# The first grouped FFN's prelude rearranged: routing in single operations beside long and short units, shared outputs two tiles at a time, later groups' rows on ScalarE

## The chip, the core and the metric

The kernel runs on one core of a Trainium2 chip. The metric is the device time of one launch in microseconds (us). The core's engines work side by side, each through its own queue: TensorE (PE; PEld is its loading of weights), VectorE (DVE), ScalarE (ACT), GpSimd (POOL) and SyncE (SP). Indirect DMAs are issued from POOL, most others from SP.

## The reference

The input x has 8 x 512 rows of 256 float32 numbers. Six layers follow one another, each on the layernorm of x and added to x. The change touches the fourth, and a part that it shares with the sixth:

```python
x = x + 0.5 * _L0_ffn_ref(_layernorm(x, axis=-1), ...)   # experts choose rows
x = x + _L0_attn_ref(_layernorm(x, axis=-1), ...)
x = x + 0.5 * _L0_ffn_ref(_layernorm(x, axis=-1), ...)
x = x + 0.5 * _L1_ffn_ref(_layernorm(x, axis=-1), ...)   # first grouped FFN
x = x + _L1_attn_ref(_layernorm(x, axis=-1), ...)
x = x + 0.5 * _L1_ffn_ref(_layernorm(x, axis=-1), ...)   # second grouped FFN
```

In `_L1_ffn_ref` a gate gives each row a softmax over 16 experts. The 16 lie in 4 groups; the 2 groups with the largest best score stay, and of their experts the row takes the 4 best, weighted by their scores. An expert computes `silu(x w1) * (x w3)` with 128 columns, times `w2`. Every row also goes through one shared expert of the same form with 256 columns (`ws1`, `ws3`, `ws2`).

## The kernel before, in words

The 4096 rows are 32 tiles of 128 rows, in 8 groups of 4 tiles. x stays on chip from layer to layer, after the third layer by way of a table in DRAM (`acc_d`). `ffn1_before` (L2129) is the first grouped FFN. All of its engines run in the order in which the program issues (a manual schedule): what is written earlier stands earlier in the queue of its engine, and every instruction waits for those ahead of it in that queue. The rows are taken in two parts: part 0 is tiles 0 to 11 (groups 0 to 2), part 1 is tiles 12 to 31 (groups 3 to 7).

The prelude, for each part:

- Mean and variance of each tile on DVE (`ln_mean`, L184 to L187); the reciprocal root for several tiles at once, for group 0 by `ln_guess` (L195, twelve small operations on DVE with no square root), for all others by `ln_range` (L178: the square root on ACT at L192, the rest on DVE at L221 to L226).
- `normal` (L1657): the normalised rows, one DVE operation a tile (L1473), into a tile that the profile calls wide.
- `columns` (L1661): 8 transposes a group on PE (tp, L1667), copied by ACT into xnT (L1670).
- `logits` (L1672): 16 small matmuls a group against the gate's weights (lg, L1675).
- `routing` (L1496): a long chain of DVE operations on the scores of the whole part (192 numbers a partition in part 0, 320 in part 1): softmax with the exponential on ACT (L1507), `topk` (L1316) for groups and for experts, counts of rows for each expert by two matmuls (pb L1543, pa L1551), the slot of each row (`slot`, L1570), the expert of each slot tile (`owner`, L1578), and the weights (`coef`, L1579 to L1582).
- `send` (L1477): 4 indirect DMAs a tile from POOL, which put each row into the slots of its experts in DRAM (slots_d, L1482). Each send waits for the last but one. Part 0 has 48, part 1 has 80.

The shared expert is cut into units that are put between these steps so that PE has work. A hidden unit (L1696, 8 matmuls of 128x512 in the profile, Silu on ACT at L1702, a product on DVE at L1707) makes half of the hidden layer of a group; an output unit (yp, L1718, 4 matmuls of 128x256) makes one tile, and DVE adds it to x (L1724). `Pump` (L2108) holds the list. Its `run(n)` issues the PE part of n units; the DVE part of each unit is issued after the PE part of the next one. `routing` is a generator that stops at each `yield`; `advance(steps, n)` (L2097) lets it go on by n stops, fewer where it says "turn". So DVE's order in routing is 3 stops (part 0) or 2 (part 1), then the DVE part of a unit, and so on.

Behind the prelude come the tile steps (L1730): the slot tiles are loaded two at a time on SP (xs, L1743), transposed (tpx, L1755), put through their expert (hs L1769, tpa L1783, yps L1791) and stored (ys_d, L1798). Loads run 4 steps ahead, and a load waits for all sends of its part. While the steps of part 1 run, the results of part 0 are gathered back and added to x. Then the attention of the fifth layer begins (its first PE instruction is tpn, L1063). The second grouped FFN (`ffn1_after`, L2276, class `Joint`) uses the same shared units behind its own tile steps, with its own routing, whose first part is done during the attention.

Of the kernel before, what the change touches and what calls it, by code (L numbers as in the profile page):

```python
# [19 lines left out]
P = 128  # L20
# [49 lines left out]
class Kernel:  # L70
# [1245 lines left out]
    def topk(self, pool, vals, n, k, hots):  # L1316


        nc = self.nc
        T = vals.shape[1]  # L1320
        left = pool.tile([P, T, n], F32, name=f"left{n}")
        nc.vector.tensor_copy(left, vals)
        for r in range(k):
            m = pool.tile([P, T], F32, name="m", bufs=2)
            nc.vector.tensor_reduce(m, left, AX.X, ALU.max)
            yield
            if n == E1:
                rank = pool.tile([P, 2, T, n], F32, name="pick")[:, 0]
            else:
                rank = pool.tile([P, T, n], F32, name=f"rank{n}")  # L1330
            nc.vector.tensor_tensor(rank, left, bc(m, 2, n), ALU.is_equal)
            nc.vector.tensor_tensor(rank, rank, bc(self.desc[:, 0:n], 1, T), ALU.mult)
            yield
            m = pool.tile([P, T], F32, name="m", bufs=2)
            nc.vector.tensor_reduce(m, rank, AX.X, ALU.max)
            nc.vector.tensor_tensor(hots[:, r], rank, bc(m, 2, n), ALU.is_equal)
            yield
            if r < k - 1:
                nc.vector.scalar_tensor_tensor(left, hots[:, r], -2.0, left, ALU.mult, ALU.add)

# [111 lines left out]
class Grouped:  # L1452
# [43 lines left out]
    def routing(self, h, lg, pool, row_psum):  # L1496
# [8 lines left out]
        nc.vector.tensor_reduce(m, lg, AX.X, ALU.max)  # L1505
        nc.vector.tensor_tensor(score, lg, bc(m, 2, E1), ALU.subtract)
        nc.scalar.activation(score, score, AF.Exp)  # L1507
        m = pool.tile([P, HT], F32, name="m", bufs=2)
# [3 lines left out]
        nc.vector.tensor_tensor(score, score, bc(m, 2, E1), ALU.mult)  # L1512
        grouped = score.rearrange("p t (g j) -> p (t g) j", g=N_GROUPS)
# [16 lines left out]
        nc.vector.tensor_tensor(view, hots[:, 0], hots[:, 1], ALU.add)  # L1530
        nc.vector.tensor_tensor(view, view, hots[:, 2], ALU.add)
        yield
        nc.vector.tensor_tensor(view, view, hots[:, 3], ALU.add)

# [8 lines left out]
        nc.tensor.matmul(pb, lhsT=k.ones, rhs=chosen.rearrange(flat), start=True, stop=True)  # L1543
        inc = pool.tile([P, E1, HT], F32, name=f"left{E1}")
# [5 lines left out]
        pa = row_psum(E1 * HT)  # L1550
        nc.tensor.matmul(pa, lhsT=k.tri, rhs=chosen.rearrange(flat), start=True, stop=True)  # L1551
# [4 lines left out]
        base = pool.tile([P, E1], F32, name="base")  # L1556
        nc.vector.tensor_tensor(base, upto, tiles, ALU.subtract)
# [6 lines left out]
        for r in range(0, TOPK, 2):  # L1564
            pick = pool.tile([P, 2, HT, E1], F32, name="pick")
            nc.vector.tensor_tensor(
                pick, hots[:, r : r + 2], bc(inc.rearrange("p e t -> p t e"), 1, 2), ALU.mult
            )
            nc.vector.tensor_reduce(where[:, r : r + 2], pick, AX.X, ALU.add)
        nc.vector.tensor_copy(self.slot[h][:, :, :HT], where)  # L1570
# [4 lines left out]
        nc.vector.tensor_scalar(past, upto, k.lanes[:, 0:1], None, ALU.is_le, ALU.add, accum_out=number)  # L1575
        row = row_psum(P)
        nc.tensor.matmul(row[0:1, :], lhsT=number, rhs=k.ident, start=True, stop=True)
        nc.vector.tensor_scalar(self.owner[h][:, : self.tiles[h]], row[0:1, : self.tiles[h]], float(E1 - 1), None, ALU.min)  # L1578
        nc.vector.tensor_tensor(hots, hots, bc(score, 1, TOPK), ALU.mult)  # L1579
        yield  # L1580
        nc.vector.tensor_reduce(self.coef[h][:, :, :HT], hots, AX.X, ALU.add)
# [74 lines left out]

    def normal(self, g):  # L1657
        for t in range(g * QT, g * QT + QT):
            self.rows(self.k.nc.vector, self.xn[:, t, :], t)
# [20 lines left out]
    def row_psum(self, cols):  # L1680
        t = self.psum.tile([P, CH], F32, name="pp", tag="lg", bufs=1)
        return t[:, :cols]

    def shared(self, g):

        nc, x = self.k.nc, self.k.x
        SC = SHARED // P

        def hidden(s):
            hs = []  # L1690

            def pe():
                for wt in (self.ws1, self.ws3):
                    hp = self.psum.tile([P, CH], F32, name="hp", tag="h", bufs=2)
                    for c in range(DC):
                        nc.tensor.matmul(  # L1696
                            hp, lhsT=wt[:, c, s * P : s * P + P], rhs=self.xnT[g][:, c, :],
                            start=(c == 0), stop=(c == DC - 1),
                        )
                    hs.append(hp)  # L1700
                sg = self.work.tile([P, CH], F32, name="sg")
                nc.scalar.activation(sg, hs[0], AF.Silu)  # L1702
                hs.append(sg)

            def dve():
                at = self.acts[g, s] = self.work.tile([P, CH], F32, name="at", bufs=4)
                nc.vector.tensor_tensor(at, hs[2], hs[1], ALU.mult)  # L1707
            return pe, dve

        def outputs(i):  # L1710
            box = []
            t = g * QT + i

            def pe():
                yp = self.psum.tile([P, D], F32, name="yp", tag="y", bufs=2)
                box.append(yp)
                for c in range(SC):
                    nc.tensor.matmul(  # L1718
                        yp, lhsT=self.acts[g, c][:, i * P : i * P + P], rhs=self.ws2[:, c, :],
                        start=(c == 0), stop=(c == SC - 1),  # L1720
                    )

            def dve():
                nc.vector.scalar_tensor_tensor(x[:, t, :], box[0], 0.5, x[:, t, :], ALU.mult, ALU.add)  # L1724
            return pe, dve

        return [hidden(s) for s in range(SC)], [outputs(i) for i in range(QT)]
# [369 lines left out]
def advance(steps, n):  # L2097

    for _ in range(n):
        what = next(steps, "end")  # L2100
        if what == "end":
            return False
        if what == "turn":
            break
    return True


class Pump:  # L2108


    def __init__(self):
        self.units, self.pending = [], None
# [4 lines left out]
    def run(self, n):  # L2117
        for _ in range(n):
            if self.units:
                pe, dve = self.units.pop(0)  # L2120
                pe()
            else:
                dve = None
            if self.pending is not None:
                self.pending()
            self.pending = dve


def ffn1_before(k, f):  # L2129
# [3 lines left out]
    with ExitStack() as ctx, k.tc.manual_schedule(engines={E.PE, E.DVE, E.Activation, E.Pool, E.SP}):  # L2133
# [3 lines left out]
        a = f.parts[0]  # L2137
        lg = f.psum.tile([P, a, E1], F32, name="lg", tag="lg", bufs=1)
        for t in range(QT):
            k.ln_mean(f.route, f.stats, t)  # L2140
        k.ln_guess(f.route, f.stats, 0, QT)
        f.normal(0)
        f.columns(0)
        k.ln_range(f.route, f.stats, QT, a - QT)
        f.normal(1)
        f.normal(2)
        f.columns(1)
        f.logits(0, lg, 0)
        f.columns(2)
        f.logits(1, lg, QT)  # L2150
        f.logits(2, lg, 2 * QT)

# [3 lines left out]
        pump.feed(groups[0][0] + groups[1][0] + groups[0][1] + groups[2][0])  # L2156
        steps = f.routing(0, lg, f.route, f.row_psum)
        pump.run(1)
        more = True
        while more:  # L2160
            more = advance(steps, 3)
            pump.run(1)
# [7 lines left out]
        k.ln_range(f.route, f.stats, a, 8)  # L2170
        pump.feed(groups[1][1] + groups[2][1])
        pump.run(2)
        f.normal(3)
        f.normal(4)
        pump.run(2)
        f.columns(3)
        k.ln_range(f.route, f.stats, a + 8, TT - a - 8)
        pump.run(2)
        f.columns(4)
        f.logits(3, lg, 0)  # L2180
        for g in range(5, 8):
            f.normal(g)
            pump.run(2)
        pump.run(len(pump.units))
        f.logits(4, lg, QT)
        pump.feed(groups[3][0])
        for g in range(5, 8):
            f.columns(g)
            pump.run(1)
            f.logits(g, lg, (g - 3) * QT)  # L2190
        pump.feed(groups[4][0] + groups[3][1])
        for g in range(5, 8):
            pump.feed(groups[g][0] + groups[g - 1][1])
        pump.feed(groups[7][1])
        steps = f.routing(1, lg, f.route, f.row_psum)
        more = True
        while more:
            more = advance(steps, 2)
            pump.run(1)
# [76 lines left out]
def ffn1_after(k, f, out):  # L2276
# [4 lines left out]
    with ExitStack() as ctx, k.tc.manual_schedule(engines={E.PE, E.DVE, E.Activation, E.Pool, E.SP}):  # L2281
# [53 lines left out]
        def hidden(g):  # L2335
            def turned():
# [3 lines left out]
            (pe, dve), rest = hs[0], hs[1:]  # L2340
            return [((lambda: (turned(), pe())), dve)] + rest, [
                (pe, (lambda dve=dve, t=g * QT + i: (dve(), done(t)))) for i, (pe, dve) in enumerate(os_)
# [111 lines left out]
```

## Time and profile before

| what | us |
|---|---|
| median of 3 runs (3877.18 to 3881.57) | 3878.12 |
| the profiled execution | 3874.62 |
| its span, first to last instruction | 3872.9 |
| start to 1761.0: three layers | 1761.0 |
| 1761.0 to 1791.5: x arrives, logits of part 0 | 30.5 |
| 1791.5 to 1824.8: routing of part 0 up to its slots | 33.3 |
| 1824.8 to 1874.8: up to the logits of part 1 | 50.0 |
| 1874.8 to 1914.2: routing of part 1 up to its slots | 39.4 |
| 1914.2 to 1940.7: remaining units | 26.5 |
| 1940.7 to 2042.2: tile steps of part 0 | 101.5 |
| 2042.2 to 2223.7: tile steps of part 1 | 181.5 |
| 2223.7 to 3682.5: attention | 1458.8 |
| 3682.5 to 3872.9: second grouped FFN, as far as it does not lie beside the attention | 190.4 |

The bounds are taken from the trace: the last logits of each part on PE, the cast of the slots on DVE, the first tpx, the last PE instruction before the wait for part 1's rows, the first tpn. The view by windows gives for each such stretch the busy time of each engine (PE, PEld, DVE, ACT, POOL, each with its number of instructions), the clock that PE was granted, the share of the DMA engines and GB/s:

```profile
1874.80:1914.20 39.40, 27.88 (x68) 14.05 (x68) 32.84 (x76) 4.14 (x6) 11.93 (x13) 0.80 0.20 71
1914.20:1940.70 26.50, 26.31 (x82) 15.90 (x83) 11.25 (x22) 2.39 (x4) 19.14 (x19) 0.93 0.25 89
1940.70:2042.20 101.50, 98.92 (x547) 87.37 (x545) 36.86 (x75) 32.72 (x75) 58.32 (x60) 1.00 0.65 210
```

In the routing of part 1 DVE is busy for 32.84 of 39.4 us; in the tile steps PE is busy nearly throughout, at full clock (1.00).

### The profile page before, as it was taken

How to read it: one execution, taken by the hardware profiler on the slowest of the kernel's cores; microseconds unless marked ns; L12 is line 12 of the kernel's file. 1: busy time of each engine (PE TensorE's matmuls, PEld its weight loads, DVE VectorE, ACT ScalarE, POOL GpSimd, SP SyncE). 2: the span in 40 equal slices, each digit the busy share in tenths (PEclk: the TensorE clock that was granted, in tenths of full speed). 3: DMA queues.
4: the chain of work that ended last, by engine and by line, in shares of the span. 5: the costliest groups of instructions: out<-in, count | busy, mean ns of one | idle time of the engine just before them, and what ended most of it. 6: DMA issues, size and time to landing. Idle time of an engine off the chain costs nothing.

```text
span 3872.9 us, 51443 instructions
## 1 busy us (share of the span) xinstructions
PE 3566.1 (92%) x18131; PEld 2230.6 (58%) x18131; DVE 1866.6 (48%) x4538; ACT 1455.6 (38%) x2928; POOL 1191.3 (31%) x1066
## 2 busy tenths in 40 slices
PE   4999997999996799996898999999999999988988
PEld 1566663555553466664587845555555555557874
DVE  7221205666654312215533556666555567546355
ACT  3222223444444222221132355555555554542321
POOL 2333324343331233321552312220000101723166
PEclk7999998999998899997898999999999999999999
DMA  5345432000113233324266500000000000235564
GB/s 186 107 129 142 131 80 86 23 17 23 29 34 95 44 72 78 73 36 135 84 217 218 183 23 28 28 28 6 1 1 1 1 1 9 73 91 185 168 197 132
DMA packets 258171, 309.30 MB, mean 80 GB/s; under 512 B 34048, under 2 KB 227968, under 8 KB 257664
## 3 DMA queue, kind: packets, MB, share of 16 engines
q1 hardware_dynamic: 182144, 177.78, 14.5%
q0 software_dynamic: 49152, 101.24, 10.5%
q10 hardware_dynamic: 26624, 27.00, 2.1%
q8 instruction: 150, 2.46, 0.3%
q14 instruction: 101, 0.83, 0.1%
HBM read 159.51 MB, written 138.02 MB: 77 GB/s over the span
## 4 chain that ended last, share of the span: by engine, by line
PE 39%; issue 8%; POOL 5%; DVE 3%; DMA 2%; ACT 1%; POOLq 0%; SPq 0%; DVEq 0%; ACTq 0%
PE sp L1104 6%; PE tp L1124 6%; PE pq L1082 6%; PE zp L1151 6%; PE pv L1071 3%; PE yp L1166 3%; PE hs L1769 2%; POOL slots_d L1482 2%; PE hp L1696 2%; POOL slots_d L1839 1%; PE yps L1791 1%; POOL yg L1991 1%; PE hs L2053 1%; PE rp L1138 1%; DMA xs<-slots_d 1%
## 5 line engine op out<-in xcount | busy, mean ns | idle before, releaser
L516 PE MATMUL hp<-exT,w 128*128 128x512 f32 x1024 | 455.8, 599 | 0.0
L547 PE MATMUL op<-w,hid 128*128 128x256 f32 x2048 | 451.9, 379 | 0.0
L1113 ACT ACTIVATE ex<-sp,nmax 128x512 f32<-128x512 f32 x512 | 344.7, 685 | 239.7 <-DVE nmax L1110 239.6
L547 PEld LDWEIGHTS op<-w,hid 128*128 128x128 f32 x2048 | 387.5, 190 | 63.5 <-issue 14.3
L552 DVE TENSOR_TENSOR ob<-op,b 128x256 f32<-128x256 f32 x128 | 54.3, 425 | 642.8 <-PE op L547 552.3
L1110 DVE TENSOR_REDUCE nmax<-sp 128x2 f32<-128x1024 f32 x256 | 301.5, 1219 | 81.4 <-PE sp L1104 81.4
L805 DVE CUSTOM_DVE_ANT_0 junk<-sp,mask 128x128 bf16<-128x128 f32 (+3 forms) x512 | 251.0, 490 | 170.3 <-PE sp L796 146.9
L526 POOL DMA_INDIRECT acc_d<-ob,idx x128 | 201.6, 1575 | 419.3 <-ACT ob L553 355.9
L516 PEld LDWEIGHTS hp<-exT,w 128*128 128x128 f32 x1024 | 194.0, 192 | 222.0 <-issue 217.4
L1124 PEld LDWEIGHTS tp<-ident,ex 128*128 128x128 f32 x2048 | 236.5, 142 | 145.8 <-issue 83.7
L520 ACT ACTIVATE hid<-hp,b 128x512 f32<-128x512 f32 x256 | 175.9, 687 | 319.8 <-PE hp L516 319.8
L1124 PE MATMUL tp<-ident,ex 128*128 128x128 f32 x2048 | 274.7, 277 | 7.4 <-ACT ex L1113 5.4
L1104 PE MATMUL sp<-qk,qk 64*128 64x512 f32 x1024 | 254.6, 616 | 0.0
L1082 PE MATMUL pq<-xnT,wide 128*128 128x512 f32 x512 | 246.3, 604 | 1.2 <-ACT xnT L246 0.8
L248 DVE COPY eT<-tp 128x512 f32<-128x512 f32 x256 | 176.9, 691 | 141.2 <-PE tp L1124 140.5
L1589 POOL DMA_INDIRECT yg<-ys_d,slot x128 | 129.9, 1015 | 363.3 <-DVE x L1602 274.4
L246 ACT COPY eT<-tp 128x512 f32<-128x512 f32 x256 | 149.6, 585 | 238.5 <-PE tp L1124 238.5
L1151 PE MATMUL zp<-eT,v 128*64 128x512 f32 x1024 | 233.9, 599 | 0.0
L487 POOL DMA_INDIRECT ex<-xn_d,idx x128 | 131.4, 1026 | 299.2 <-DVE idx L478 265.0
L553 ACT ACTIVATE ob<-ob,gate 128x256 f32<-128x256 f32 x128 | 65.0, 508 | 414.0 <-DVE ob L552 414.0
L848 ACT ACTIVATE ex<-st 128x1024 f32<-128x1024 f32 x160 | 155.1, 1022 | 97.0 <-PE st L841 97.0
L1053 POOL TENSOR_TENSOR x<-x,xn 128x1024 f32<-128x1024 f32 x8 | 18.9, 2360 | 545.7 <-DVE xn L1048 545.7
(427 smaller groups left out, 5942.0 us busy)
## 6 DMA issues: line engine op xcount, KB each, us to landing
xs<-slots_d SPq DMA_DIRECT2D x149, 256.0 KB, 2.8
ys_d<-ys SPq DMA_DIRECT2D x149, 256.0 KB, 2.4
w<-in_W SPq DMA_DIRECT2D x32, 1024.0 KB, 5.3
slots_d<-zero ACTq DMA_DIRECT2D x7, 2304.0 KB, 12.8
w_sb<-in_w SPq DMA_DIRECT2D x24, 512.0 KB, 7.9
xn_d<-xn SPq DMA_DIRECT2D x16, 512.0 KB, 3.0
acc_d<-x SPq DMA_DIRECT2D x16, 512.0 KB, 4.6
x<-acc_d SPq DMA_DIRECT2D x16, 512.0 KB, 7.8
```

Source lines behind the costliest of these rows:

```text
L248: self.nc.vector.tensor_copy(out, in_)
L516: nc.tensor.matmul(hp, lhsT=w1[:, c, f * P : f * P + P], rhs=exT[e][:, c, h * CH : h * CH + CH], start=(c == 0), stop=(c == DC - 1),)
L520: nc.scalar.activation(hid[h][:, f, :], hp, AF.Gelu, bias=b1[:, e, f : f + 1])
L526: inst = nc.gpsimd.indirect_dma_start(out=acc_d[:, :], out_offset=bass.IndirectOffsetOnAxis(ap=idx[:, e, st : st + 1], axis=0), in_=ob, in ...
L547: nc.tensor.matmul(op, lhsT=hid[h][:, f, i * P : i * P + P], rhs=w2[:, f, :], start=(f == 0), stop=(f == FC - 1),)
L805: nc.vector.tensor_tensor_reduce(out=junk[:, :wd], in0=sps[h // 2][:, h % 2, at : at + wd], in1=mask[:, S - wd :], scale=1.0, scalar=NEG, ...
L1082: nc.tensor.matmul(pp, lhsT=(wq, wk)[a][:, k, c * P : c * P + P], rhs=xnT[b][:, k, :], start=(k == 0), stop=(k == DC - 1),)
L1104: nc.tensor.matmul(sp[:, j, :], lhsT=q[r, qt * P : qt * P + P], rhs=k[r, :], start=True, stop=True)
L1110: nc.vector.tensor_reduce(nmax, sp, AX.X, ALU.max, negate=True)
L1113: nc.scalar.activation(ex[:, j, :], sp[:, j, :], AF.Exp, bias=nmax[:, j : j + 1], accum_out=ch["sums"][:, qt, j : j + 1],)
L1124: nc.tensor.transpose(tp[:, k, :], ch["ex", qt][:, j, k * P : k * P + P], self.ident)
L1151: nc.tensor.matmul(zp[DK1 * j : DK1 * j + DK1, :], lhsT=v[b, h][:, k, at : at + DK1], rhs=ch["eT"][:, j, k, :], start=(k == 0), stop=(k == ...
```

## The change

- `routing` and `topk` stop after nearly every DVE operation ("op"). `advance` counts these stops only when asked to (`fine`); the second grouped FFN does not ask. The number of operations between two units is now that of the unit: 6 after a hidden unit, 2 after an output unit (`room`).
- An output unit makes two tiles in one PSUM tile, and DVE adds both at once: 16 units in place of 32. This holds for the second grouped FFN too.
- The two count matmuls of routing are issued together (pa has its own place in PSUM); the weights of the four ranks are made by 4 + 4 smaller operations in place of 1 + 1.
- Group 0's hidden units go ahead of group 1's columns. All reciprocal roots come from `ln_guess`.
- The rows of groups 4 to 7 are made on ACT by two activations a tile (`shifted`: x minus the mean, then times the reciprocal root); group 3's stay on DVE. All 32 activations are issued ahead of group 3's `columns`.
- Units are dealt out anew: 10 for routing of part 0, one with each of groups 3 to 7, and 15 left for the routing of part 1.

```diff
         nc.vector.tensor_copy(left, vals)
+        yield "op"
...
             nc.vector.tensor_tensor(rank, left, bc(m, 2, n), ALU.is_equal)
+            yield "op"
             nc.vector.tensor_tensor(rank, rank, bc(self.desc[:, 0:n], 1, T), ALU.mult)
             yield
             m = pool.tile([P, T], F32, name="m", bufs=2)
             nc.vector.tensor_reduce(m, rank, AX.X, ALU.max)
+            yield "op"
             nc.vector.tensor_tensor(hots[:, r], rank, bc(m, 2, n), ALU.is_equal)
...
         nc.vector.tensor_reduce(m, lg, AX.X, ALU.max)
+        yield "op"
         nc.vector.tensor_tensor(score, lg, bc(m, 2, E1), ALU.subtract)
         nc.scalar.activation(score, score, AF.Exp)
+        yield "turn"
...
         pb = row_psum(E1 * HT)
         nc.tensor.matmul(pb, lhsT=k.ones, rhs=chosen.rearrange(flat), start=True, stop=True)
+        pa = row_psum(E1 * HT, "pa")
+        nc.tensor.matmul(pa, lhsT=k.tri, rhs=chosen.rearrange(flat), start=True, stop=True)
+        yield "turn"
         inc = pool.tile([P, E1, HT], F32, name=f"left{E1}")
         nc.vector.tensor_tensor_scan(inc.rearrange(flat), carry.rearrange(flat), pb, 0.0, ALU.mult, ALU.add)
         tiles_i = pool.tile([P, E1], I32, name="tiles_i")
         nc.vector.tensor_scalar(tiles_i, inc[:, :, HT - 1], float(P - 1), None, ALU.add)
         nc.vector.tensor_scalar(tiles_i, tiles_i, 7, None, ALU.arith_shift_right)
...
-        pa = row_psum(E1 * HT)
-        nc.tensor.matmul(pa, lhsT=k.tri, rhs=chosen.rearrange(flat), start=True, stop=True)
+        yield "op"
...
         nc.vector.tensor_scalar(past, upto, k.lanes[:, 0:1], None, ALU.is_le, ALU.add, accum_out=number)
+        yield "turn"
         row = row_psum(P)
         nc.tensor.matmul(row[0:1, :], lhsT=number, rhs=k.ident, start=True, stop=True)
+        yield "turn"
         nc.vector.tensor_scalar(self.owner[h][:, : self.tiles[h]], row[0:1, : self.tiles[h]], float(E1 - 1), None, ALU.min)
-        nc.vector.tensor_tensor(hots, hots, bc(score, 1, TOPK), ALU.mult)
+        for r in range(TOPK):
+            nc.vector.tensor_tensor(hots[:, r], hots[:, r], score, ALU.mult)
+            yield "op"
         yield
-        nc.vector.tensor_reduce(self.coef[h][:, :, :HT], hots, AX.X, ALU.add)
+        for r in range(TOPK):
+            nc.vector.tensor_reduce(self.coef[h][:, r, :HT], hots[:, r], AX.X, ALU.add)
+            yield "op"
         nc.vector.tensor_scalar(self.coef[h][:, :, :HT], self.coef[h][:, :, :HT], 0.5, None, ALU.mult)
...
+    def shifted(self, g):
+        nc, (mv, rstd) = self.k.nc, self.stats
+        t0 = g * QT
+        down = self.route.tile([P, QT], F32, name="down", bufs=2)
+        nc.vector.tensor_scalar(down, mv[:, t0 : t0 + QT, 0], -1.0, None, ALU.mult)
+        for t in range(t0, t0 + QT):
+            out = self.xn[:, t, :]
+            nc.scalar.activation(out, self.k.x[:, t, :], AF.Identity, bias=down[:, t - t0 : t - t0 + 1])
+            nc.scalar.mul(out, out, rstd[:, t : t + 1])
+
...
-    def row_psum(self, cols):
-        t = self.psum.tile([P, CH], F32, name="pp", tag="lg", bufs=1)
+    def row_psum(self, cols, name="pp"):
+        if name == "pa":
+            t = self.psum.tile([P, CH], F32, name="pa", tag="a", bufs=1)
+        else:
...
-                yp = self.psum.tile([P, D], F32, name="yp", tag="y", bufs=2)
+                yp = self.psum.tile([P, 2, D], F32, name="yp", tag="y", bufs=2)
                 box.append(yp)
-                for c in range(SC):
-                    nc.tensor.matmul(
-                        yp, lhsT=self.acts[g, c][:, i * P : i * P + P], rhs=self.ws2[:, c, :],
-                        start=(c == 0), stop=(c == SC - 1),
-                    )
+                for u in range(2):
+                    at = (i + u) * P
+                    for c in range(SC):
+                        nc.tensor.matmul(
+                            yp[:, u, :], lhsT=self.acts[g, c][:, at : at + P], rhs=self.ws2[:, c, :],
+                            start=(c == 0), stop=(c == SC - 1),
+                        )
 
             def dve():
-                nc.vector.scalar_tensor_tensor(x[:, t, :], box[0], 0.5, x[:, t, :], ALU.mult, ALU.add)
+                both = x[:, t : t + 2, :]
+                nc.vector.scalar_tensor_tensor(both, box[0], 0.5, both, ALU.mult, ALU.add)
             return pe, dve
 
-        return [hidden(s) for s in range(SC)], [outputs(i) for i in range(QT)]
+        return [(*hidden(s), 6) for s in range(SC)], [(*outputs(i), 2) for i in range(0, QT, 2)]
...
-def advance(steps, n):
-
-    for _ in range(n):
+def advance(steps, n, fine=False):
+
+    while n > 0:
         what = next(steps, "end")
         if what == "end":
             return False
         if what == "turn":
             break
+        if what != "op" or fine:
+            n -= 1
     return True
...
-        self.units, self.pending = [], None
+        self.units, self.pending, self.room = [], None, 6
...
-                pe, dve = self.units.pop(0)
+                pe, dve, self.room = self.units.pop(0)
...
+        stats = f.route, f.stats
         lg = f.psum.tile([P, a, E1], F32, name="lg", tag="lg", bufs=1)
-        for t in range(QT):
-            k.ln_mean(f.route, f.stats, t)
-        k.ln_guess(f.route, f.stats, 0, QT)
+        pump = Pump()
+        groups = [f.shared(g) for g in range(TT // QT)]
+
+        def means(g):
+            for t in range(g * QT, g * QT + QT):
+                k.ln_mean(*stats, t)
+
+        def beside(steps):
+            more = True
+            while more:
+                pump.run(1)
+                more = advance(steps, pump.room, True)
+
+        means(0)
+        k.ln_guess(*stats, 0, QT)
         f.normal(0)
         f.columns(0)
-        k.ln_range(f.route, f.stats, QT, a - QT)
+        pump.feed(groups[0][0])
+        means(1)
+        pump.run(1)
+        means(2)
+        pump.run(1)
+        k.ln_guess(*stats, QT, a - QT)
         f.normal(1)
-        f.normal(2)
         f.columns(1)
         f.logits(0, lg, 0)
+        f.normal(2)
         f.columns(2)
+        pump.feed(groups[1][0] + groups[0][1] + groups[2][0] + groups[1][1] + groups[2][1])
+        pump.run(1)
         f.logits(1, lg, QT)
         f.logits(2, lg, 2 * QT)
-
-        pump = Pump()
-        groups = [f.shared(g) for g in range(TT // QT)]
-
-        pump.feed(groups[0][0] + groups[1][0] + groups[0][1] + groups[2][0])
-        steps = f.routing(0, lg, f.route, f.row_psum)
-        pump.run(1)
-        more = True
-        while more:
-            more = advance(steps, 3)
-            pump.run(1)
+        means(3)
+        means(4)
+        beside(f.routing(0, lg, f.route, f.row_psum))
         for t in range(a):
             f.send(0, t, f.xn[:, t, :])
         load, step, total, first = f.tile_steps()
             load(j)
 
         lg = f.psum.tile([P, f.parts[1], E1], F32, name="lg", tag="lg", bufs=1)
-        k.ln_range(f.route, f.stats, a, 8)
-        pump.feed(groups[1][1] + groups[2][1])
-        pump.run(2)
+        for g in range(5, 8):
+            means(g)
+            pump.run(1)
+        k.ln_guess(*stats, a, TT - a)
         f.normal(3)
-        f.normal(4)
-        pump.run(2)
-        f.columns(3)
-        k.ln_range(f.route, f.stats, a + 8, TT - a - 8)
-        pump.run(2)
-        f.columns(4)
-        f.logits(3, lg, 0)
-        for g in range(5, 8):
-            f.normal(g)
-            pump.run(2)
         pump.run(len(pump.units))
-        f.logits(4, lg, QT)
-        pump.feed(groups[3][0])
-        for g in range(5, 8):
+        for g in range(4, 8):
+            f.shifted(g)
+        for g in range(3, 8):
             f.columns(g)
+            pump.feed({3: groups[3][0][:1], 4: groups[3][0][1:], 5: groups[4][0], 6: groups[3][1][:1], 7: groups[3][1][1:]}[g])
             pump.run(1)
             f.logits(g, lg, (g - 3) * QT)
-        pump.feed(groups[4][0] + groups[3][1])
-        for g in range(5, 8):
+        pump.feed(groups[5][0] + groups[4][1])
+        for g in range(6, 8):
             pump.feed(groups[g][0] + groups[g - 1][1])
         pump.feed(groups[7][1])
-        steps = f.routing(1, lg, f.route, f.row_psum)
-        more = True
-        while more:
-            more = advance(steps, 2)
-            pump.run(1)
+        beside(f.routing(1, lg, f.route, f.row_psum))
         for t in range(f.parts[1]):
             f.send(1, t, f.xn[:, a + t, :])
...
-            (pe, dve), rest = hs[0], hs[1:]
-            return [((lambda: (turned(), pe())), dve)] + rest, [
-                (pe, (lambda dve=dve, t=g * QT + i: (dve(), done(t)))) for i, (pe, dve) in enumerate(os_)
+            (pe, dve, room), rest = hs[0], hs[1:]
+            return [((lambda: (turned(), pe())), dve, room)] + rest, [
+                (pe, (lambda dve=dve, t=g * QT + 2 * i: (dve(), done(t), done(t + 1))), room)
+                for i, (pe, dve, room) in enumerate(os_)
```

## Prediction

> **What bounds the kernel now.** I first read the page: its span, and the part that follows back the chain that ended last.
>
> ```profile
> span 3872.9 us, 51443 instructions
> ...
> PE 39%; issue 8%; POOL 5%; DVE 3%; DMA 2%; ACT 1%; POOLq 0%; SPq 0%; DVEq 0%; ACTq 0%
> ```
>
> The median of the runs is 3878.12 us and the profiled execution took 3874.62, 3.5 less. I sum against 3874.62 and carry the difference over to the median. TensorE (PE) carries the chain for most of the kernel, and a delay there is a delay of the end; so the question is where, in the stage that is changed (about 1761 to 2224 us), PE stands still. Next view: that chain in order of time, around 2045 us.
>
> ```profile
> 2042.36 0.98 POOL slots_d L1482
> 2043.35 0.19 issue
> 2043.54 0.03 POOLq L1589
> 2043.57 0.20 issue
> 2043.77 2.42 DMA slots_d<-wide,slot
> ...
> 2046.33 2.81 DMA xs<-slots_d
> 2049.14 0.04 issue
> 2049.18 1.11 PE tpx L1755 x4
> ```
>
> The 80 sends of part 1 hold the chain, not PE: the last begins at 2043.77, and the first expert tile of part 1 can be loaded only when all rows are there (2049.18). PE's timeline says how much slack there is:
>
> ```profile
> 2041.83 0.38 PE L1783 MATMUL tpa<-ident,as 128*128 128x128 f32 x2
> 2049.18 1.11 PE L1755 MATMUL tpx<-ident,xs 128*128 128x128 f32 x4 [6.97 <-DMA xs<-slots_d]
> ```
>
> PE is idle for 7 us there. So what decides is when the sends can begin, that is when `slots(1)`, the cast at L1570 of part 1's routing, is done (1914.2; first send 1914.46), and how long 80 of them take. PE work saved before them gains nothing. In the POOL timeline the 21 intervals up to 1944.81, beside the prelude, take 1.445 us each, the next 47, beside tile steps with their loads and stores, (2028.06 - 1944.81) / 47 = 1.771, and the last 11, when loads are blocked, 1.428. From the first to the last: 129.3 us. Now the prelude by tens of microseconds:
>
> ```profile
> 1780.00:1790.00 10.00, 10.00 (x49) 10.00 (x49) 0.00 (x0) 2.97 (x4) 0.00 (x0) 0.50 1.16 307
> 1830.00:1840.00 10.00, 3.74 (x8) 2.58 (x9) 9.28 (x35) 0.21 (x1) 7.38 (x8) 0.63 0.29 106
> 1900.00:1910.00 10.00, 5.19 (x12) 2.83 (x12) 8.52 (x21) 0.00 (x0) 0.00 (x0) 0.72 0.01 2
> ```
>
> VectorE (DVE, third busy number) fills 1830 to 1840 and most of the routing at 1900, with PE (first) half empty; PE fills 1780 to 1790 at half clock (0.50). The prelude is a chain from DVE to PE to DVE.
>
> **The change part by part**, along that chain.
>
> *Start, up to the logits of groups 0 to 2: +5.4.* Now these end at 1791.5. Group 0's hidden units move in front of group 1's columns. Their weights land at about 1776 (issued 1770.04; neighbouring loads took 4.8 to 6.1). 16 matmuls: some 4 at 0.855 (cold, as at 1791), 12 at 0.43, so to 1784.6. DVE's product for the first unit stands ahead of `ln_guess`: it ends at 1782.4; the guess is 12 operations at 0.20 = 2.4, four row normalisations at 0.33 = 1.3, so group 1's transposes start at 1786.5, not 1777.65. In return PE is warm: a group's logits 1.69 instead of 3.23 to 3.44. Transposes 2 x 0.92, one unit 3.44, three logits 5.1: 1796.9. Bounds +3 to +8.
>
> *Routing of part 0: +2.5.* Now 33.3 us to `slots(0)` (1824.8), of which DVE does 4.4 for units, 7.8 is waits, and 21.1 is routing. After: ten units with a 128x512 operation of 0.685 = 6.9. The shared addition of two tiles at once is a row of this trace by its shape (L1707: 685 ns; two of L1724: 836). 21.1 + 6.9 + the same 7.8 = 35.8. Finer interleaving can take at most the waits; but the largest, 5.2 for the exponential, stays, since it again stands behind a unit's Silu. Bounds 0 to +5. `slots(0)`: 1832.7. The 48 sends of part 0 slide by the same 8 and end at 1898, long before they are missed.
>
> *From there to the logits of group 7: +10.3.* Now 50.0 us (to 1874.8), with row normalisation of later groups on DVE between PE's transposes. After, in DVE's order: `hots` by score 4 x 0.39, coefficients 4 x 0.39, owner 0.6 (3.7 in all, nothing new); means of groups 5 to 7, 12 pairs at 0.53 = 6.4; guess 2.4; group 3's rows 1.3: 1846.5. Then ScalarE (ACT) gets 16 tiles by two activations. No row of before does exactly this; the nearest is the 128x256 activation with a per-partition operand:
>
> ```profile
> L553 ACT ACTIVATE ob<-ob,gate 128x256 f32<-128x256 f32 x128 | 65.0, 508 | 414.0 <-DVE ob L552 414.0
> ...
> L246 ACT COPY eT<-tp 128x512 f32<-128x512 f32 x256 | 149.6, 585 | 238.5 <-PE tp L1124 238.5
> ```
>
> I take 508: 32 x 0.508 = 16.3. Half of the 585-ns copy would make 9.4, 0.6 each 19.2. All 32 are issued ahead of group 3's xnT copies, which PE waits for; no other work covers them, since the units are used up by then (nine after 1797: 3 x 3.44 + 6 x 1.72 = 20.6, so to 1818). After its own transposes PE idles from 1847.7 until the first copy, 1862.8 + 0.6 = 1863.4. Then 4 x 0.92 transposes + 5 x 1.69 logits + 4 x 3.44 + 1.72 for units = 27.6, and some 2 for the cold clock: 1893.0. Bounds +4 to +15. On DVE the same 16 tiles cost 16 x 0.33 = 5.3: the gain on DVE is less than the new row on ACT.
>
> That ACT does not overtake is in its timeline: the subtraction for the exponential ended at 1792.3, its table load stood behind Silu, which waited 8.35 for PE:
>
> ```profile
> 1795.18 0.60 ACT L1702 ACTIVATE sg<-hp 128x512 f32<-128x512 f32 x1 [8.35 <-PE hp L1696]
> 1795.80 1.28 ACT L1507 ACT_TABLE_LOAD   x1
> ```
>
> The Trainium skill, "TensorE: Matmul & The Clock Gate", section "Architectural detail: the array is 16× 32×32, not 1× 128×128", says the same, that ScalarE's queue is strictly first in, first out; it speaks against this step. If ACT could let the copies pass, the step would be about 13 less.
>
> *Routing of part 1: +1.1.* Now 39.4 us from the first maximum (1874.83) to `slots(1)`: 5.6 for units, about 5 waits, 28.9 routing. After: 15 units are left, 15 x 0.69 = 10.4, so 39.3 with no wait at all. Units against room: a long one 3.44 of PE beside 6 x 0.52 + 0.69 = 3.8 of DVE, a two-tile one 1.72 beside 1.73: this fits, I add 1.2. 40.5. Bounds 0 to +5. `slots(1)`: 1893.0 + 40.5 = 1933.5, **19.3 us later** than now. Unlike now, hardly a unit is left after it (before, PE had 26 us of them, to 1940.7): PE is ready for tile steps at about 1935, 6 earlier, for nothing.
>
> *Sends of part 1: 0.* 2 or 3 intervals at 1.445, then 47 or 48 at 1.771 (the loads run as far ahead as before), 28 or 29 at 1.43: 129. First tile at 1933.8 + 129.3 + 5.4 = 2068.5; PE, done with part 0 at 1935 + 101.5 = 2036.5, idles some 32 us instead of 7. What follows is unchanged work.
>
> *Removed table loads* (three of 1.283, two of them for the square root) were ACT's, beside DVE's chain; the guesses of 2.4 that stand for square roots are counted above. Nothing.
>
> *Second grouped FFN: -1.5.* It uses two-tile units too; routing there is unchanged. Its end is 1.3 us a gather on POOL. Only behind the last gather does a one-tile unit remain (PE 1.15 from 3868.69, addition to 3870.28); it ends sooner by about that. Bounds -4 to +2.
>
> **Sum:** 5.4 + 2.5 + 10.3 + 1.1 + 0 - 1.5 = +17.8: 3874.6 becomes 3892.4, and on the median 3878.1 + 17.8 = **3896**.
>
> One rule about the clock. The rows show 0.50 from 1761 to 1795.1 although PE was busy for 10.00 of 10 in 1780 to 1790, with transposes and 16-column logits; it rose 3.7 us after the dense 128x512 matmuls began. The Trainium skill, same page, section "🔬 Part 1: The HAM clock gate (the "warmup" mystery)", says that one busy window of about 3.4 us frees the clock. By the rule the cold start costs an estimated 1.7 where I took 2; the rows differ for sparse work, and I go by them.
>
> **Rivals.**
>
> *Not slower (0.12).* The sends no longer slow down beside tile steps. Place: the intervals at 1.771. Price: 79 x 1.44 = 113.8 from 1933.8, last send 2047.6, first tile 2053.0, +3.8; with -1.5, +2.3: 3880. PE has then ended part 0 before (2036.5), so it does not decide. It comes within 0.2% (7.8 us, about what a measurement of this kernel can tell from no change) when those 48 intervals fall to 1.55, and to nothing only at a mean of 1.41, under any stretch measured. For it: POOL's own 0.98 leaves room. Against: the loads and stores are the same.
>
> *ACT cheaper (0.15).* At 9.4 instead of 16.3, or as much of it hidden: 17.8 - 6.9 = +11, 3889.
>
> *Much slower (0.11).* The clock stays at half through groups 3 to 7, as in 1780 to 1790, because logits lie between units: 27.6 more, less the 2: +43, 3921. Against: in 1859 to 1870 now, unit and logits alternate at full clock. Or the sends take 1.771 throughout: 79 x 1.771 = 139.9, 10.6 more, +28.
>
> *The change does not do what it says.* If DVE still waits for units in routing, as now (5 instead of 1.2), it is +22: inside the forecast's own range.
>
> **How the numbers follow.** Forecast 0.62, with 3884 to 3908 as its own range from the bounds; the rivals as given. Faster by over 0.2% needs the first rival plus the low bounds of two steps: 0.05. Within 0.2%: the rest of that rival, 0.07, and the cheapest ACT, 0.04: 0.11. Slower: 0.84. The range 3883 to 3910 leaves out most of the first rival and the clock.
>
> **What would show it.** Group 1's transposes near 1786; `slots(0)` near 1833; a block of 32 activations of 0.5 us with PE idle until group 3's copies; last logits near 1893; `slots(1)` near 1934; additions of 128x512 at 0.69; a wait of PE's tpx for xs of 25 to 34 us in place of 7. Wrong if `slots(1)` comes before 1922, or if the sends take under 118 us.

## The result, and the profile after

The changed kernel takes 3898.43 us (median of 4 runs, 3894.3 to 3904.9) beside 3878.61 us before (4 runs): a ratio of 1.0056, 95% interval 1.0044 to 1.0068, so 19.8 us slower. The forecast was 3896.

The profiled execution took 3894.3 us. Its span, and the shares by engine of the chain that ended last:

```profile
span 3892.3 us, 51456 instructions
...
PE 42%; issue 6%; POOL 3%; DMA 3%; DVE 2%; ACT 1%; POOLq 0%; DVEq 0%; SPq 0%; ACTq 0%
```

The chain in order of time, at the place that was read before. Times are from the start of this trace, in which x arrives at 1761.7 (1765.1 before; the same kernel's traces differ by a few us here).

```profile
2065.50 2.42 DMA slots_d<-wide,slot
...
2068.06 2.85 DMA xs<-slots_d
2070.91 0.04 issue
2070.96 1.12 PE tpx L1791 x4
```

The last send of part 1 again holds the first expert tile of that part. PE's timeline there:

```profile
2036.48 0.38 PE L1819 MATMUL tpa<-ident,as 128*128 128x128 f32 x2
2070.96 1.12 PE L1791 MATMUL tpx<-ident,xs 128*128 128x128 f32 x4 [34.10 <-DMA xs<-slots_d]
```

PE now waits 34 us in place of 7. It ended part 0 earlier and had nothing to do: close to the slack that was foretold (some 32). Where the start of the sends was delayed is seen in the windows (PE, PEld, DVE, ACT, POOL busy, then PE's clock):

```profile
1780.00:1790.00 10.00, 9.74 (x46) 5.92 (x45) 9.00 (x36) 3.34 (x6) 0.00 (x0) 1.00 1.16 308
1830.00:1840.00 10.00, 0.59 (x2) 0.09 (x2) 8.84 (x37) 0.00 (x0) 6.90 (x7) 0.50 0.22 80
1850.00:1860.00 10.00, 0.25 (x1) 0.25 (x2) 0.17 (x1) 9.67 (x22) 7.47 (x8) 0.50 0.29 105
1900.00:1910.00 10.00, 10.00 (x32) 5.81 (x31) 9.21 (x20) 1.19 (x2) 0.00 (x0) 1.00 0.31 98
```

The first and last show what the change does well: PE at full clock in 1780 to 1790 (0.50 before), and in the routing of part 1 PE busy for 10.00 and DVE for 9.21 of 10 us. The third is new: of these three engines only ACT works, 9.67 of 10, while PE and DVE stand still and PE's clock is at 0.50. (POOL's 7.47 are the sends of part 0.) ACT's timeline at the end of that block, and PE's on both sides of it:

```profile
1858.19 0.49 ACT L1684 ACTIVATE wide<-x,down 128x256 f32<-128x256 f32 x1
1858.72 0.51 ACT L1685 ACTIVATE wide<-wide,rstd 128x256 f32<-128x256 f32 x1
1859.13 1.05 ACT L1700 COPY xnT<-tp 128x512 f32<-128x512 f32 x2
```

```profile
1842.93 2.29 PE L1697 MATMUL tp<-ident,wide 128*128 128x128 f32 x8 [12.23 <-DVE wide L1477]
1859.75 5.43 PE L1729 MATMUL hp<-xnT,ws_sb 128*128 128x512 f32 x8 [14.53 <-ACT xnT L1700]
```

Group 3's transposes are done at 1845; the copies that PE needs start at 1859.13, right behind the 32nd activation.

### The profile page after: what moved, and what is told of

Same layout as the page of the kernel before. It is cut to its first block, busy times and chain, and to the rows that moved or that the text cites. A ratio compares the mean times of both kernels' runs of the same rounds, so it can differ in the third digit from the quotient of the medians.

```text
span 3892.3 us, 51456 instructions
## 1 busy us (share of the span) xinstructions
PE 3551.9 (91%) x18131; PEld 2219.5 (57%) x18131; DVE 1859.1 (48%) x4512; ACT 1466.2 (38%) x2954; POOL 1191.4 (31%) x1066
## 4 chain that ended last, share of the span: by engine, by line
PE 42%; issue 6%; POOL 3%; DMA 3%; DVE 2%; ACT 1%; POOLq 0%; DVEq 0%; SPq 0%; ACTq 0%
PE sp L1104 6%; PE tp L1124 6%; PE pq L1082 6%; PE zp L1151 6%; PE hs L1805 3%; PE pv L1071 3%; PE yp L1166 3%; PE hp L1729 2%; PE yps L1827 2%; POOL slots_d L1875 1%; PE yp L1753 1%; PE hs L2089 1%; PE tpx L1791 1%; POOL yg L2027 1%; DMA yg<-ys_d,slot 1%
```

## The experiments

Twelve kernels ran in three series of four, each series on one chip, beside the kernel before. In the first two series the kernel before itself took 3960 us and the traces show stops that no trace before or after them has (told below), so those kernels are compared with each other, and stretch by stretch only where no sends run; the third series is like the first result (3874.83 us before, 9 runs).

I measure stretches from the arrival of x, in us: L0 is the start of the routing of part 0 (the first DVE row on its logits), S0 its slots, L1 and S1 the same for part 1.

### First series: undo one part each

**Rows of groups 4 to 7 on VectorE (e1).**

```diff
         for g in range(4, 8):
-            f.shifted(g)
+            f.normal(g)
```

> The changed kernel with the rows of groups 4 to 7 made by VectorE again (one operation a tile, 0.33 us each) in place of the 32 activations; all else as changed. Theory (the activations cost what they hold up: group 3's copies stand behind them in ScalarE's queue and TensorE waits 14.5 us): that wait goes, VectorE's 5.3 us lie beside TensorE's work on group 3, the last logits and the slots of part 1 come 14 us earlier, 3898 becomes about 3884. Rival (VectorE is what bounds this stretch, so that work taken off it was a gain): the wait shrinks only to about 5 and part of it comes back behind it, 3889 to 3893. Rival (the sends are bound elsewhere): no change, 3898.

Measured 3956.07 us, ratio to before 0.9988 (0.9959 to 1.0017). The wait of 14.5 us is gone: PE goes from group 3's transposes to its unit within 2.1 us (1848.77 to 1850.89). But then ACT stops, with nothing that the trace names as its releaser (it writes `remote`), and S0 to L1 takes 77 us:

```profile
1871.10 0.58 ACT L1700 COPY xnT<-tp 128x512 f32<-128x512 f32 x1 [16.96 <-remote]
1874.61 0.58 ACT L1700 COPY xnT<-tp 128x512 f32<-128x512 f32 x1 [2.92 <-remote]
```

No verdict on the total from this run.

**The activations behind the copies of the group before (e2).**

```diff
-        for g in range(4, 8):
-            f.shifted(g)
         for g in range(3, 8):
             f.columns(g)
+            if g < 7:
+                f.shifted(g + 1)
```

> The changed kernel with the same 32 activations on ScalarE, but eight of them, those of group g+1, issued behind the copies of group g, in place of all 32 ahead of group 3's copies. Theory (the place in the queue is what costs, not the engine): group 3's copies come 15 us earlier, TensorE has 5 to 6 us of work a group beside 4 us of activations, so nearly the same gain as with the rows on VectorE: 3884 to 3886. Rival (ScalarE is too slow for the rows wherever they stand): each group waits for its rows, 4 groups of about 2 to 4 us, 3890 to 3898.

3953.17 us, 0.9989 (0.9964 to 1.0014). Here too PE goes on at once (transposes 1846.31, unit 1848.43, group 4's transposes 1854.32) with the rows still on ACT, before stops of the same kind begin:

```profile
1846.31 2.29 PE L1697 MATMUL tp<-ident,wide 128*128 128x128 f32 x8 [12.27 <-DVE rstd L213]
1848.43 4.36 PE L1729 MATMUL hp<-xnT,ws_sb 128*128 128x512 f32 x8
```

So the 14.5 us wait came from the place in the queue, not from the engine; whether ACT keeps up over four groups is not seen behind the stops.

**Group 0's units late (e3).**

```diff
-        pump.feed(groups[0][0])
         means(1)
-        pump.run(1)
         means(2)
-        pump.run(1)
...
-        pump.feed(groups[1][0] + groups[0][1] + ...
+        pump.feed(groups[0][0] + groups[1][0] + groups[0][1] + ...
```

> The changed kernel with group 0's two hidden units no longer ahead of group 1's columns but first in the list of units, so that they fall beside the routing of part 0. Theory (they delay the logits of part 0 by 5 to 6 us, but in routing they cost VectorE some waits): the last logits of part 0 some 5 us earlier, routing up to 3 us longer, 3898 becomes 3894 to 3896. Rival (the warm clock that they bring pays for them): the logits run at half clock again and nothing is won, 3897 to 3900.

3955.66 us, 0.9981 (0.9950 to 1.0012). The stretch in question lies before any send. L0 comes at 29.1 in place of 32.5 (e1, same prelude up to there), S0 at 66.7 in place of 68.4. So the early units cost some 3.4 us at the logits and 1.7 at the slots. These are rough: the eleven traces whose start is that of the changed kernel have L0 at 31.1 to 33.4, and the ten of them with its routing of part 0 too have S0 at 68.0 to 70.9, so the gain lies between 2.0 and 4.3 at the logits and between 1.3 and 4.2 at the slots, and whether routing gives any of it back is not shown. The clock takes part of the gain: group 0's logits take 3.43 us here and 1.86 in the changed kernel.

**All 15 units behind the sends (e4)**, on top of e1:

```diff
-        beside(f.routing(1, lg, f.route, f.row_psum))
+        for _ in f.routing(1, lg, f.route, f.row_psum):
+            pass
```

> The rows on VectorE as in the first kernel, and besides the routing of part 1 runs with no unit beside it: all 15 units are issued behind the sends. Theory (the start of part 1's sends decides, and units before it gain nothing): routing takes 29 to 30 us in place of 42.4, the slots come 26 us earlier than in the changed kernel, the units fill TensorE beside the sends, 3898 becomes 3870 to 3874, below the kernel before. Rival (TensorE's work decides as soon as it is moved behind): TensorE idles some 30 us in routing and then has 36 us of units and 101.5 us of tile steps, it ends part 0 about 12 us later than the sends allow, 3882 or more.

4011.54 us, 1.0131 (1.0084 to 1.0178): slower, against my theory. Its first half nearly holds: L1 to S1 takes 32.0 us (29 to 30 expected). The rest does not: the units and first tile steps beside the sends stand still, ACT for 63.1 us at the longest.

### Second series: the same, with the changed kernel as yardstick

> The changed kernel itself, unaltered, as the yardstick for the kernels run with it on the same chip. The first series ran on a chip on which the kernel before took 3960 us and ScalarE and VectorE stood still for 12 to 31 us at a time with no releaser in the trace; the changed kernel was not among its runs. Both theories: on a chip without such stops 20 us (0.5%) above the kernel before; on one with them within 1% of it, and the trace shows the stops.

> The rows of groups 4 to 7 on VectorE, again. Theory (the copies behind the 32 activations cost TensorE 14.5 us): 14 us below the changed kernel on this chip, unless unexplained stops fall into the stretch. Rival (VectorE bounds this stretch): 5 to 9 us below it.

> The activations behind the copies of the group before, again. Theory (the place in the queue costs, not the engine): 12 to 14 us below the changed kernel on this chip. Rival (ScalarE is too slow for the rows wherever they stand): 0 to 8 us below it.

> The rows on VectorE and all 15 units behind the sends of part 1, again. Theory (the start of part 1's sends decides): on a chip without the stops 24 to 28 us below the changed kernel, under the kernel before. Rival (work moved beside the sends is held up there, as the first series seemed to show with stops of 17 to 63 us on ScalarE and VectorE during the sends): above the changed kernel on any chip.

| kernel | us | ratio to before, 95% | L0 | S0 | L1 | S1 |
|---|---|---|---|---|---|---|
| changed (f0) | 3954.86 | 0.9958 (0.9926 to 0.9990) | 32.4 | 68.3 | 160.3 | 202.4 |
| rows on DVE (f1) | 3950.85 | 0.9960 (0.9932 to 0.9988) | 32.9 | 70.5 | 157.5 | 199.5 |
| activations later (f2) | 3954.02 | 0.9978 (0.9945 to 1.0012) | 31.1 | 68.7 | 155.3 | 196.8 |
| units after, rows on DVE (f4) | 4011.08 | 1.0120 (1.0088 to 1.0152) | 33.4 | 70.9 | 157.5 | 189.5 |

S0 to L1 takes 87 to 92 us in all four, where the first trace of the changed kernel has 59.7. Stops lie there, beside the 48 sends of part 0, and in f0 they end with them: PE's transposes of group 4 are recorded at 1872.00, the last send begins at 1899.4, and ACT's copy of these transposes at 1901.24:

```profile
1901.24 0.58 ACT L1700 COPY xnT<-tp 128x512 f32<-128x512 f32 x1 [31.87 <-remote]
```

The stops are not only there. In the second grouped FFN, beside POOL's indirect gathers, ACT waits in f0 for up to 13.3 us in the same way, and the stretch from the attention to the end takes 1675 to 1689 us in the eight kernels of these two series, beside 1648 to 1659 in the six other traces. Of the 70 us between the two traces of the changed kernel, 32 lie between S0 and L1 and 32 in that last stretch.

The wait of 14.5 us is swallowed by that, so the total does not tell e1's edit from e2's or from none. In f4 the same happens beside the sends of part 1 (us in total, times, longest):

```profile
ACT xT L246 <- remote: 60.1, 1, 60.1
...
DVE x L1760 <- remote: 31.9, 3, 17.6
```

So on these chips, at that time, PE's work beside sends was held up, and moving 15 units there costs 60 us (4011.08 - 3950.85, f1, from which f4 differs by that alone; in the first series, e4 against e1, 55). That fits that the changed kernel, with no unit left beside the sends of part 1, is there a little faster than the kernel before, which has 26 us of them; there is no trace of the kernel before in that condition, so this is argued, not shown.

One number of f4 bears on a rival of the prediction. Its 80 sends run beside units and a few tile steps that stand still, so beside few loads and stores (the DMA engines move 93 to 107 GB/s from 1960 to 2060, and 204 in the tile steps of the changed kernel), and take 109.9 us from first to last, 1.39 each (110.4 in e4); with tile steps running beside them they take 127 to 134 us in every other kernel.

### Third series: the activations, without sends beside them

> The kernel before, unaltered, for a trace of it on a chip like those of the two series so far. Theory (TensorE's releases arrive late while sends run, so that on such a chip TensorE's work beside sends costs far more than its own time): between the slots of part 0 and the logits of part 1, and in the 26 us of units behind the slots of part 1, the trace shows stops that the first trace of this kernel does not have, 30 us or more in all. Rival (these chips are slower throughout): every stretch is longer by about 2%, the three layers ahead of the prelude too.

A single run: 3882.03 us, no stop without a named releaser. The condition was over, so its expectation could not be tried. The stretches are those of the first trace within 4 us: L0 26.5, S0 60.0, L1 106.9, S1 144.9 (first trace 26.5, 59.7, 109.7, 148.9); the sends of part 1 take 129.3 us in both.

**Changed kernel, sends of part 0 held back until part 1's weights are done (g1).**

```diff
+        hold = f.route.tile([P, QT], F32, name="hold")
+        nc.gpsimd.tensor_scalar(hold, f.coef[1][:, 0, 0:QT], 1.0, None, ALU.mult)
+        for t in range(a):
+            f.send(0, t, f.xn[:, t, :])
...
```

(The sends of part 0 and the first loads move from behind the routing of part 0 to just ahead of part 1's sends. The new operation on POOL reads the weights of part 1, and the sends stand behind it in POOL's queue.)

> The changed kernel with the sends of part 0 held back until the weights of part 1 are done, so that nothing is sent while the prelude runs. Yardstick for the next kernel. Both theories: the sends of both parts run one after the other from the slots of part 1 on, the tile steps begin some 65 us later, the total is 20 to 60 us above the changed kernel, and the prelude shows no stops: logits of part 1 at 125 to 130 us after x arrives, slots at 168 to 172, as in the first trace of the changed kernel.

**The same with the rows on VectorE (g2)**, the edit of e1 on top.

> The same with held sends, but the rows of groups 4 to 7 on VectorE in place of the 32 activations. Theory (the copies behind the 32 activations cost TensorE 14.5 us and nothing hides it): logits and slots of part 1 come 13 to 15 us earlier than with the activations, and as much is seen in the total. Rival (VectorE bounds this stretch, the activations take work off it): 5 to 9 us. Rival (it is hidden elsewhere): less than 3.

g1 takes 3972.32 us (3968.2 to 3976.45, 5 runs; ratio to before 1.0252, 1.0238 to 1.0266), 74 above the changed kernel where 20 to 60 were expected, g2 3949.07 (3947.65 to 3953.16; 1.0193, 1.0179 to 1.0207). What PE waited for in the prelude, first g1, then g2 (us in total, times, longest):

```profile
PE tp L1697 <- DVE wide L1477: 26.7, 3, 14.4
PE hp L1729 <- ACT xnT L1700: 14.4, 1, 14.4
PE pp L1592 <- DVE past L1589: 9.9, 2, 5.3
```

```profile
PE tp L1697 <- DVE wide L1477: 26.7, 3, 14.4
PE pp L1592 <- DVE past L1589: 9.9, 2, 5.3
PE pp L1552 <- DVE chosen L1541: 8.0, 1, 8.0
```

The one line that goes is the wait for the copies. (Of each answer the first three lines are shown; what follows is the same in both but for the wait for the weights ws_sb, 4.1 and 3.4.) S0 to L1 falls from 60.3 to 43.8 us, by 16.5: the wait of 14.4, and 2 from the clock, since PE no longer cools down (group 3's unit takes 4.49 us in place of 6.38). L1 to S1 stays (42.0 and 42.1). The theory holds, with somewhat more than the 13 to 15 us that it gave, and both rivals fall: VectorE's rows come back nowhere. The total falls by 23 us, more than the 16.5 that I can place; of the two profiled executions' 23.9, 2 are in the sends and 5 in the stretch from the attention on, which the edit does not touch. What makes those 7 stays open; the last stretch differs by up to 11 us (1648 to 1659) among the undisturbed traces.

**Coarse stops in routing (g3).**

```diff
-                more = advance(steps, pump.room, True)
+                more = advance(steps, n)
```

(n is 3 in part 0 and 2 in part 1.)

> The changed kernel with the routing advanced by the coarse stops again, 3 in part 0 and 2 in part 1 between two units; all else as changed. Theory (the routing of part 1 is bound by the sum of VectorE's work, units' parts included; finer stops only take waits, of which there are few): from the last logits to the slots 40 to 44 us, as with fine stops (42.1). Rival (fine stops keep VectorE from waiting for long units): 47 us or more, and the total is longer by the same.

3897.67 us, 1.0060 (1.0045 to 1.0075), as good as the changed kernel's 1.0056. L1 to S1 is 43.5 (42.1 with fine stops): the theory. What I had not expected: L0 to S0 is 30.6 with coarse stops and 35.8 with fine ones (35.8 to 37.6 in the ten traces that have them there). The units and operations of DVE in that stretch are the same in both. In part 0 the operations are short (0.36), so with 2 of them to an output unit DVE comes back before PE has made it, and waits. VectorE's waits in that stretch, of the changed kernel:

```profile
DVE at L1740 <- PE hp L1729: 4.2, 2, 2.9
...
DVE x L1760 <- PE yp L1753: 1.8, 5, 0.4
DVE at L1740 <- ACT sg L1735: 1.7, 1, 1.7
```

With coarse stops the last two lines are not there, nor is a wait of 0.7 for the count matmul, and DVE's waits for hp are 3.8. The finer interleaving costs 5 us in part 0 and gains 1.4 in part 1. The attention begins 3.9 us earlier than in the changed kernel (478.7 and 482.6 from the arrival of x), but the total does not show it: in these two traces the stretch behind it is some 3 us longer.

## Why the prediction was right

Step by step, from the profiled executions of before and after, each measured from the arrival of x:

| step | predicted | measured |
|---|---|---|
| start, up to the routing of part 0 (L0) | +5.4 | 32.2 - 26.5 = +5.7 |
| routing of part 0 (to S0) | +2.5 | 35.8 - 33.2 = +2.6 |
| up to the logits of part 1 (L1) | +10.3 | 59.7 - 50.0 = +9.7 |
| routing of part 1 (to S1) | +1.1 | 42.1 - 39.2 = +2.9 |
| sends of part 1, first to last | 0 | 133.6 - 129.3 = +4.3 |
| first tile of part 1 to the attention | 0 | 173.2 - 174.5 = -1.3 |
| attention and second grouped FFN | -1.5 | 1648.1 - 1649.2 = -1.1 |

They add up to +22.8, where +17.8 was forecast; in this trace x arrives 3.4 us earlier, which leaves the 19.4 between the two spans. So in this pair of traces the total is closer than the steps by luck: nothing in the change moves the arrival of x, which lies between 1761.7 and 1771.4 in the traces of this case.

- The *bound* was right: the end of part 1's sends decides, and their start is what the change moved. PE, ready for tile steps 5 us earlier in relation to x (170.7 against 175.6), gains nothing from it and waits 34.1 us (some 32 in the sum, 25 to 34 as the sign).
- The *activations* were the largest term and rightly read, from a row of another stage. They take 0.49 and 0.51 us (508 ns was taken). The block is a little shorter than foretold, 15.0 us in place of 16.3, since each tile's first activation starts 0.41 us after the second of the tile before. g1 and g2 show that, with the sends held back, nothing covers it.
- The *two-tile additions* cost what the row by shape said: 0.689 us.
- *Routing of part 1* was mis-sized by 1.8: 15 operations of units with 10.3 us, as counted, but 3.5 us of waits (for yp 1.9, for hp 1.6) in place of 1.2.
- *The sends* were mis-sized by 4.3. The slow intervals were put at 47 or 48, as before. There are 54, at (2028.90 - 1931.93) / 54 = 1.80. The likely reason, argued and not tested, is that the tile steps and their loads now begin with the first send, and the first steps on a cold clock (0.50 from 1932 to 1940), where it was 1.00 before, behind the units:

```profile
1932.40:2036.90 104.50, 102.22 (x547) 89.62 (x546) 39.95 (x84) 32.91 (x75) 59.18 (x60) 0.96 0.64 204
```

  The same 547 matmul rows took 101.5 us before, at a clock of 1.00. How much of the 4.3 would come again is not shown: the three other changed kernels of the third series have 131.3 to 133.4 us from first to last send, 2 to 4 above the kernel before.
- *The tail* looks as described: the last additions follow the last gather at once, with no unit of PE between them. That this is worth 1.5 is not shown. From the start of the last gather to the end of the last addition it is 5.6 us in place of 6.1, and the whole stretch from the attention on, where -1.1 stands, varies by ten times as much among the undisturbed traces.

Two steps were right in sum only. In the routing of part 0, 7.8 us of waits were carried over because the exponential's 5.2 would stay. There are 7.7 for units and 0.7 for the count matmul, but that one is not among them (the view above), and g3, without the fine stops, has 4.6 us of these waits less. Ten units were counted, and nine fall into the stretch. And of the start's +5.7 some 3.4 are the early units (e3, between 2.0 and 4.3); the rest, in which the unit between the logits and the longer guess lie, was not separated.

Of the rivals, "not slower" needed sends at a mean of 1.41 us; f4 shows 1.39 with few tile steps beside them, so such sends are possible, but in the changed kernel the mean is 133.6 / 79 = 1.69. That 1.41 lay "under any stretch measured" was misread: in the trace of before the 48 sends of part 0 take 1.37 each (64.3 / 47). "ACT cheaper" and the half clock did not happen.

## What to carry over

Where engines run in a written order, work moved to an idle engine is not free: ask what stands behind it in that engine's queue and who waits for that. Here 5 us of rows on VectorE became 15 us in front of a copy that TensorE needed; the same activations behind that copy, in e2, did not hold TensorE up. And before work is packed in front of a long transfer, see whether it could lie beside it: after the change TensorE has its units done and waits 34 us, and the start of the transfer is what counts. That moving all 15 units there gains is not shown: e4 and f4 did it, and were 55 and 60 us slower in the disturbed series; it was not run in the third.

Stops in a routing loop should follow the length of the operations: 2 operations to a unit fit at 0.5 us each (part 1), not at 0.36 (part 0).

## What was not expected of the hardware

In the first two series ScalarE stood still for up to 63 us (e4) and VectorE for up to 31 (e2) at a time beside POOL's indirect sends, and for shorter times beside its indirect gathers, in f0 although the matmuls that ScalarE waited for had long been recorded. TensorE was idle meanwhile: 0.00 of the 20 us from 1880 to 1900 in f0, at a clock of 0.50. There the wait reached to the end of the sends. In the third series, and in the first traces, nothing of the kind is seen, with the same sends at 1.35 to 1.8 us each. The two disturbed series ran on two chips, and the third on one of these, so it is not the chip alone. What brings the condition about was not tried.

The sends of part 1 take 1.80 us an interval beside the tile steps' loads and stores, 1.46 behind them, and 1.39 in f4 with few of them.

The same transposes and 16-column logits that ran at half clock from 1780 to 1790 before, and again in e3 (1780 to 1784), ran at full clock in the changed kernel, behind 16 dense matmuls of 128x512: the clock rose while these ran, from 0.50 up to 1777 to 1.00 from 1778 on, and stayed there through the small ones that followed, to 1795.

Outside the disturbed series no version here was shown to be faster than the kernel before (in the second, f0 and f1 are 0.4% below it). The changed kernel with its rows on VectorE (e1) should come near it, by an estimated 16 to 23 us less than 3898 as g2 has it; it was only measured in the disturbed series, where it is level with the changed kernel.
